# Reciprocals of the softmax row sums: spread by a DRAM round trip instead of on VectorE

## The chip, the cores and the metric

One core of one Trainium2 chip runs the whole program. The metric is the device time of one execution in microseconds (us). The kernel before takes 999.54 us (median of three runs, 999.5 to 1000.05).

## What is computed

The reference is one cross-attention block with adaptive layer norm, 16 images, 1024 query rows, 64 context rows and 16 heads of 32 features, all in float32:

```python
xq  = ada_ln(x_q,  t_vec, Wss_q,  bss_q)      # (1 + scale) * layernorm + bias
xkv = ada_ln(x_kv, t_vec, Wss_kv, bss_kv)
q   = (xq @ Wq + bq).reshape(B, Lq, 16, 32)   # B 16, Lq 1024, H 512
k, v = (xkv @ Wkv + bkv) split in 16 heads    # Lkv 64
attn = softmax(q k^T / sqrt(32))
return x_q + (attn v).reshape(B, Lq, 512) @ Wp + bp
```

The change concerns the division of softmax: every head and query row has one sum of exponentials, and `attn v` is multiplied with its reciprocal.

## The kernel before

**Tiles.** The 16 x 1024 query rows are cut into NB = 32 blocks of 512 rows (TB). Block `i` passes through a pipeline that is spread over several iterations of one loop (`for i in range(3, NB - 2)`, 27 iterations). The order of the instructions on each engine is written out by hand; each engine executes its own in that order. An iteration works at once on: scores and exponentials of block `i`; the multiplication with v, the division and half of the output projection of block `a = i - 1`; the rest of the projection of `b = i - 2`; the query projection of `n = i + 1`; the scaling of the features of `f = i + 2`; layer norm and turning of `i + 3` and the statistics of `i + 4`.

**Scores and weights.** 128 partitions hold 4 groups `c` of 32 context rows, the columns are 4 heads `r` in the group by 512 query rows. TensorE writes the scores `ps` (L738), VectorE takes a maximum over 32x32 blocks (L755) and spreads it to the tile `mb` (L784), GpSimd subtracts (L797), ScalarE takes the exponential (L808).

**The row sums.** GpSimd adds the two halves of the exponentials to the tile `sum` (`total`, L858). Its buffer has the tag `vb` and is one of its kind. VectorE sums it by blocks to `lt` (`row_total`, L863), 128 partitions by 64 columns: partition 32c + a and column (r, j) hold the sum of head (c, r), query row 32j + a.

**The reciprocals.** `inverse_rows` (L875) takes the reciprocal of `lt` (L878), writes it to DRAM (L881), and reads it back in four pieces (L883) such that partition 32r + a holds what belongs to head position `r`, as 64 columns (c, j), tile `vr`. One iteration later `spread_rows` (L886, the instruction at L891) makes the 128x2048 tile `vb` of it on VectorE: a 32x32 transpose of each column repeated 32 times. `divided` (L915) multiplies `po`, the weights times v that TensorE left in PSUM, with `vb` and leaves `ot`, of which the output projection is made.

**The queues.** Almost all DMAs are issued by SyncE (SP), in program order. After `total(i)` these are, in an iteration: the next block's x (L119), two copies `p<-s` (`swapped`, L813, each 32 partitions of 8 KB), twelve moves `xt<-ht` (L382, each 32 partitions of 2 KB) of block `i + 3`, then the write and the four reads of `inverse_rows`, then the last four moves, the next block's residual `r` (L126) and two stores of a finished block (L1118). The moves bring the turned features to the tile `xt`. Of that tile ScalarE scales one chunk after another in the next iteration (`scale_features(f, ...)`, L442), and each chunk has all 128 partitions, thus needs all sixteen moves. In ScalarE's order the first of the four scales stands ahead of `biased(a, 2)` (L1031) and of both exponentials (L808) of block `i`.

Of the kernel before, what the change touches and what calls it, by code (L numbers as in the profile page):

```python
# [9 lines left out]
F32 = mybir.dt.float32  # L10
# [5 lines left out]
P = 128  # L16
# [4 lines left out]
def cross_attention_block(  # L21
# [18 lines left out]
    nc = tc.nc  # L40
# [5 lines left out]
    NC = H // P  # L46
    HPC = P // DH
    TB = 512
    NT = TB // P
    BPB = LQ // TB  # L50
    NB = B * BPB
# [8 lines left out]
    qpool = ctx.enter_context(tc.tile_pool(name="qpool", bufs=2))  # L60
# [5 lines left out]
    dram = ctx.enter_context(tc.tile_pool(name="dram", bufs=2, space=bass.MemoryType.DRAM))  # L66
# [518 lines left out]
    def quarter_products(i, v, first):  # L585

        x, t, k = feature_quarter(i, v), t_quarters, 1 if v == 7 else 0
        w = lambda m, c: weight_quarter(v, m, c)
        s = lambda k: weight_quarter_sum(v, k)
        if first:  # L590
            qa["q", k] = bank(f"pq_{i}_{v}", k)
            todo = (
                (0, w(0, 0), x[:, 0, 0, :]),
                (1, s(0), t[:, 0]),
                (2, s(2), t[:, 1]),
                (3, s(1), t[:, 2]),
            )
        else:
            todo = (
                (0, w(0, 1), x[:, 0, 1, :]),  # L600
                (1, s(3), x[:, 1, 1, :]),
                (2, w(1, 1), t[:, 3]),
            )
        for q, lhsT, rhs in todo:
            nc.tensor.matmul(  # L605
                qa["q", k][:, q * P : (q + 1) * P],
                lhsT=lhsT,
                rhs=rhs,
                start=first and q == 0,
                stop=True,  # L610
                skip_group_check=True,
            )
# [150 lines left out]
    def copied(i, z, e):  # L763
        nc.scalar.copy(s_tiles[i, z][:, 2 * e : 2 * e + 2, :], s_banks[i, z][e])  # L764
# [69 lines left out]
    vb_tiles = {}  # L834
# [40 lines left out]
    def inverse_rows(i):  # L875

        lt = lt_tiles.pop(i)
        nc.vector.reciprocal(lt, lt)  # L878
        v = small.tile([P, NC, NJ], F32, tag="vr", name=f"vr_{i}", bufs=2)
        d = dram.tile([NC, 32, HPC, NJ], F32, tag="lt", name=f"ltd_{i}")  # L880
        nc.sync.dma_start(d.rearrange("c a r j -> (c a) r j"), lt)  # L881
        for r in range(HPC):
            nc.sync.dma_start(v[32 * r : 32 * r + 32], d[:, :, r, :].rearrange("c a j -> a c j"))  # L883
        vt_rows[i] = v

    def spread_rows(i, cs=range(NC)):  # L886
        n = len(cs)
        v = vt_rows[i][:, cs[0] : cs[-1] + 1, :].rearrange("p c j -> p (c j)")
        if cs[0] == 0:
            vb_tiles[i] = qpool.tile([P, NC, TB], F32, tag="vb", name=f"vb_{i}", bufs=1)  # L890
        nc.vector.transpose(  # L891
            vb_tiles[i][:, cs[0] : cs[-1] + 1, :].rearrange("p c q -> p (c q)"),
            v.unsqueeze(2).to_broadcast([P, n * NJ, 32]),
        )
        if cs[-1] == NC - 1:
            vt_rows.pop(i)
# [198 lines left out]
    def added(i, n):  # L1095

        m, o = {1: (0, 0), 2: (0, 0), 6: (0, 1), 7: (1, 1), 5: (1, 1), 4: (0, 1), 3: (1, 0)}[n]
        r = r_tiles[i][:, 2 * m : 2 * m + 2, o * HO : (o + 1) * HO]
        k = acc_bank(i, n)
        if i < NB - 1 or n not in (1, 6, 5, 3):  # L1100
            a = acc[k].rearrange("p (t h) -> p t h", t=2)
        if i == NB - 1:

            for ts in ((0,), (1,)) if n in (1, 6, 5, 3) else ((0, 1),):
                src = z_halves[ts[0]][:, :HO].unsqueeze(1) if len(ts) == 1 else a
                ts = slice(ts[0], ts[-1] + 1)
                nc.vector.tensor_add(r[:, ts, :], src, r[:, ts, :])  # L1107
                if n == 5 and ts.start == 0:
                    continue
                if n == 5:  # L1110
                    ts = slice(0, 2)
                if n in (2, 3, 4, 5):
                    dst = rows_of(out, i)[:, 2 * m : 2 * m + 2, o * HO : (o + 1) * HO]
                    nc.sync.dma_start(dst[:, ts, :], r[:, ts, :])
            return
        nc.vector.tensor_add(r, a, r)  # L1116
        if n in (3, 4):
            nc.sync.dma_start(  # L1118
                rows_of(out, i)[:, 2 * m : 2 * m + 2, :], r_tiles[i][:, 2 * m : 2 * m + 2, :]
            )  # L1120
# [298 lines left out]
    context_out("B", "v", 7)  # L1419
    hidden(4, (2,))  # L1420
    inverse_rows(0)
    maximum(1, 1, 0)
    feature_sums(2, nc.gpsimd, (0,))
# [96 lines left out]
    added(0, 7)  # L1520
    feature_sums(3, nc.gpsimd, (3,))
    inverse_rows(1)
    added(0, 6)
    again(1, 1)
# [55 lines left out]
    move(5, ks=(2,))  # L1580
    row_total(2)
    inverse_rows(2)
    move(5, ks=(3,))
    feature_sums(4, nc.gpsimd, (3,))
    load_residual(2)

    for i in range(3, NB - 2):
        a, b, n, f = i - 1, i - 2, i + 1, i + 2
# [37 lines left out]
        product(b, 3)  # L1626
        quarter_adds(n, 7)
        quarter_products(n, 7, False)
        spread_rows(a)
        added(b, 4)  # L1630
        if i < NB - 3:
            hidden(i + 3, (3,))
# [72 lines left out]
    y, z = NB - 2, NB - 1  # L1705
# [29 lines left out]
    query_added(z, 4)  # L1735
    added(y - 2, 7)
    copied(y, 1, 0)
    spread_rows(y - 1)
    copied(y, 1, 1)
    subtract(y, zs=(1,))  # L1740
    query_out(z, 3)
# [127 lines left out]
```

## Time and profile before

| | before |
|---|---|
| median of the runs | 999.54 us |
| the profiled execution | 999.71 us, of it the span 997.9 us |
| TensorE (PE) busy | 984.6 us, 99% of the span |
| VectorE (DVE) busy | 896.2 us, 90% |
| GpSimd (POOL) busy | 894.6 us, 90% |
| ScalarE (ACT) busy | 778.1 us, 78% |
| the spread at L891, 33 times | 73.8 us of VectorE, 2238 ns each |
| DMA of the hardware queue (q1) | 163.93 MB, 55.3% of 16 engines |

Busy time is the time in which an engine had an instruction of the program; the idle time in front of an instruction is shown in brackets with what ended it. "SPq" rows are the issues of DMAs: their duration is the time that the issue took, not the transfer. A DMA's landing is told by the profile as a median from issue to the completion of its last byte. Matmul ends are modelled, so a busy TensorE must be read beside the regularity of its starts.

### The profile page before, as it was taken

How to read it: one execution, taken by the hardware profiler on the slowest of the kernel's cores; microseconds unless marked ns; L12 is line 12 of the kernel's file. 1: busy time of each engine (PE TensorE's matmuls, PEld its weight loads, DVE VectorE, ACT ScalarE, POOL GpSimd, SP SyncE). 2: the span in 40 equal slices, each digit the busy share in tenths (PEclk: the TensorE clock that was granted, in tenths of full speed). 3: DMA queues.
4: the chain of work that ended last, by engine and by line, in shares of the span. 5: the costliest groups of instructions: out<-in, count | busy, mean ns of one | idle time of the engine just before them, and what ended most of it. 6: DMA issues, size and time to landing. Idle time of an engine off the chain costs nothing.

```text
span 997.9 us, 20561 instructions
## 1 busy us (share of the span) xinstructions
PE 984.6 (99%) x7465; PEld 762.7 (76%) x7465; DVE 896.2 (90%) x1318; ACT 778.1 (78%) x1165; POOL 894.6 (90%) x690
## 2 busy tenths in 40 slices
PE   7999999999999999999999999999999999999997
PEld 7888777787777877877778778777787787777756
DVE  6787889999999999999999999999999999987786
ACT  3788778888888888888888888888888888876620
POOL 3668899999999999999999999999999999999681
PEclk9999999999999999999999999999999999999999
DMA  9665736555655455466555554665555555444422
GB/s 314 233 195 149 191 90 178 152 164 182 188 177 175 154 176 150 148 187 188 180 176 150 175 158 141 187 187 181 173 153 174 147 155 183 147 136 133 142 81 97
DMA packets 115188, 165.77 MB, mean 166 GB/s; under 512 B 34920, under 2 KB 46464, under 8 KB 113168
## 3 DMA queue, kind: packets, MB, share of 16 engines
q1 hardware_dynamic: 114704, 163.93, 55.3%
q8 instruction: 59, 0.97, 0.4%
q0 software_dynamic: 384, 0.54, 0.2%
q14 instruction: 41, 0.34, 0.1%
HBM read 79.47 MB, written 34.60 MB: 114 GB/s over the span
## 4 chain that ended last, share of the span: by engine, by line
PE 93%; DVE 3%; DMA 1%; issue 1%; SPq 0%; ACT 0%; DVEq 0%; ACTq 0%
PE pp L1086 36%; PE pq L534 30%; PE pq L605 10%; PE ps L738 7%; PE po L936 6%; PE pv_B L534 1%; PE pk_B L534 1%; PE pk_A L534 1%; PE pv_A L534 1%; DMA vr<-ltd 0%; DMA ltd<-lt 0%; DVE vb L891 0%; DVE m L755 0%; DVE xk_sums_A L493 0%; DVE l L826 0%
## 5 line engine op out<-in xcount | busy, mean ns | idle before, releaser
L797 POOL TENSOR_TENSOR s<-s,mb 128x2048 f32<-128x2048 f32 x64 | 290.6, 4563 | 20.3 <-DVE mb L784 12.3
L1086 PE MATMUL pp<-w_p_sb,ot 128*128 128x256 f32 x740 | 174.8, 380 | 1.2 <-DVE ot L915 1.2
L764 ACT COPY s<-ps 128x1024 f32<-128x1024 f32 x128 | 129.3, 1012 | 58.2 <-PE ps L738 46.5
L755 DVE TRANSPOSE_TENSOR_REDUCE m<-ps 128x32 f32<-128x1024 f32 x128 | 152.6, 1228 | 12.0 <-PE ps L738 11.5
L1086 PEld LDWEIGHTS pp<-w_p_sb,ot 128*128 128x128 f32 x740 | 138.6, 190 | 19.8 <-issue 1.8
L858 POOL TENSOR_TENSOR sum<-s,p 128x2048 f32<-128x2048 f32 x30 | 136.3, 4544 | 1.5 <-ACT p L808 1.5
L645 ACT ACTIVATE qt<-pq,bias_t 128x256 f32<-128x256 f32 x256 | 107.2, 471 | 34.2 <-PE pq L605 27.8
L1116 DVE TENSOR_TENSOR r<-pp,r 128x512 f32<-128x512 f32 x183 | 120.3, 669 | 13.6 <-ACT xt L442 5.8
L534 PE MATMUL pq<-xt,w_q_sums 128*128 128x256 f32 x512 | 123.8, 385 | 0.0
L534 PEld LDWEIGHTS pq<-xt,w_q_sums 128*128 128x128 f32 x512 | 95.1, 190 | 34.4 <-issue 22.6
L1086 PE MATMUL pp<-WT,ot 128*128 128x256 f32 x492 | 118.4, 384 | 0.0
L1086 PE MATMUL pp<-WT,s 128*128 128x256 f32 x488 | 116.1, 381 | 1.2 <-DVE r L1107 0.8
L817 ACT ACTIVATE s<-s 32x2048 f32<-32x2048 f32 x60 | 114.6, 1910 | 1.4
L1086 PEld LDWEIGHTS pp<-WT,ot 128*128 128x128 f32 x492 | 91.1, 190 | 18.3 <-issue 3.6
L327 ACT ACTIVATE x<-x,rstdq 128x512 f32<-128x512 f32 x128 | 94.8, 807 | 5.0 <-POOL rstdq L304 5.0
L1086 PEld LDWEIGHTS pp<-WT,s 128*128 128x128 f32 x488 | 88.3, 191 | 13.4 <-DVE r L1107 1.2
L442 ACT ACTIVATE xt<-xt,ss_q 128x512 f32<-128x512 f32 x124 | 94.4, 808 | 1.1 <-DMA xt<-ht 1.0
L915 DVE TENSOR_TENSOR ot<-po,vb 128x1024 f32<-128x1024 f32 x62 | 73.0, 1218 | 15.9 <-PE po L936 15.6
L493 POOL TENSOR_TENSOR xt_sums<-xt 128x512 f32<-128x512 f32 x64 | 81.2, 1268 | 6.2 <-ACT xt L442 6.0
L286 DVE BATCH_NORM_STATS2 bs<-x 128x6 f32<-128x512 f32 x128 | 85.3, 666 | 0.0
L891 DVE STREAM_TRANSPOSE vb<-vr 128x2048 f32<-128x2048 f32 (+1 forms) x33 | 73.8, 2238 | 6.2 <-DMA vr<-ltd 6.0
L357 DVE STREAM_TRANSPOSE ht<-x 128x512 f32<-128x512 f32 x124 | 77.5, 679 | 0.4 <-issue 0.2
(224 smaller groups left out, 1964.5 us busy)
## 6 DMA issues: line engine op xcount, KB each, us to landing
x<-in_x_dram SPq DMA_DIRECT2D x32, 1024.0 KB, 5.5
r<-in_x_dram SPq DMA_DIRECT2D x32, 1024.0 KB, 5.7
xt<-ht SPq DMA_DIRECT2D x488, 64.0 KB, 2.0
out_dram<-r SPq DMA_DIRECT2D x60, 512.0 KB, 4.8
p<-s SPq DMA_DIRECT2D x60, 256.0 KB, 3.8
wss_kv<-in_L_xcond_Wss_kv_dram SPq DMA_DIRECT2D x4, 512.0 KB, 7.2
wss_q<-in_L_xcond_Wss_q_dram SPq DMA_DIRECT2D x4, 512.0 KB, 11.6
vr<-ltd SPq DMA_DIRECT2D x128, 8.0 KB, 1.7
```

Source lines behind the costliest of these rows:

```text
L327: nc.scalar.activation(dst, src, AF.Identity, bias=rstd[:, 1, j : j + 1], scale=rstd[:, 0, j : j + 1])
L442: nc.scalar.activation(xt[:, :, c, :], xt[:, :, c, :], AF.Identity, scale=ss["q"][:, c, b : b + 1], bias=ss["q"][:, NC + c, b : b + 1],)
L534: nc.tensor.matmul(out_, lhsT=lhsT, rhs=rhs, start=new and m == 0 and c == 0, stop=c == HC - 1, skip_group_check=True,)
L605: nc.tensor.matmul(qa["q", k][:, q * P : (q + 1) * P], lhsT=lhsT, rhs=rhs, start=first and q == 0, stop=True, skip_group_check=True,)
L645: nc.scalar.activation(dst, src, AF.Identity, bias=bq_t[:, o : o + 1])
L755: nc.vector.tensor_reduce(m_tiles[i][:, z, 2 * e : 2 * e + 2, :], s_banks[i, z][e].rearrange("p r (j a) -> p r j a", a=32), AX.X, ALU.max, ...
L764: nc.scalar.copy(s_tiles[i, z][:, 2 * e : 2 * e + 2, :], s_banks[i, z][e])
L797: eng.tensor_tensor(s_tiles[i, z], s_tiles[i, z], mb_tiles[i], ALU.subtract)
L817: nc.scalar.activation(s_tiles[i, 0][at + 32 : at + 64], raw_tiles[i][at : at + 32], AF.Exp, scale=SCALE)
L858: nc.gpsimd.tensor_tensor(t, s_tiles[i, 0], s_tiles[i, 1], ALU.add)
L1086: nc.tensor.matmul(to, lhsT=rows[:, c, t * P : (t + 1) * P], rhs=cols[:, c, :], start=n == 2 and (i, 2) not in seeded and t == 0 and c == ...
L1116: nc.vector.tensor_add(r, a, r)
```

## The change

For blocks 2 to 29 `inverse_rows` now takes another way, and `spread_rows` is not called for them (in the loop, and once behind it). VectorE transposes the 128x64 reciprocals in 32x32 blocks, so that a partition holds 32 query rows that lie side by side. One DMA writes them to DRAM as whole rows of 512 floats, 256 pieces of 128 bytes. Four DMAs read them back: each takes the four rows (2 KB each) of one head position `r` and writes them to all 32 partitions of its quarter of `vb`. `vb` is thus filled at the end of iteration `i` by DMA, and not in iteration `i + 1` by VectorE. Blocks 0, 1, 30 and 31 keep the old way.

```diff
         v = small.tile([P, NC, NJ], F32, tag="vr", name=f"vr_{i}", bufs=2)
+        if 2 <= i < NB - 2:
+            t = v.rearrange("p c j -> p (c j)")
+            nc.vector.transpose(t, lt.rearrange("p r j -> p (r j)"))
+            d = dram.tile([2, NC, 2, TB], F32, tag="lb", name=f"lb_{i}")
+            nc.sync.dma_start(
+                d.rearrange("k c e (j a) -> (c e j) k a", a=32),
+                t.rearrange("p (k a) -> p k a", k=2),
+            )
+            vb = vb_tiles[i] = qpool.tile([P, NC, TB], F32, tag="vb", name=f"vb_{i}", bufs=1)
+            for r in range(HPC):
+                row = d[r // 2, :, r % 2, :].unsqueeze(0)
+                nc.sync.dma_start(vb[32 * r : 32 * r + 32], row.to_broadcast([32, NC, TB]))
+            return
         d = dram.tile([NC, 32, HPC, NJ], F32, tag="lt", name=f"ltd_{i}")
...
         quarter_products(n, 7, False)
-        spread_rows(a)
         added(b, 4)
...
     copied(y, 1, 0)
-    spread_rows(y - 1)
     copied(y, 1, 1)
```

What the instruction order becomes is shown at three places, around the iteration that works on block 14. On VectorE, where the spread stood, before (`pq_7` is the query projection of the next block, `r_4253` a block whose projection is being added, `po` the weights times v of block 13):

```order
L624 TENSOR_TENSOR pq_7_4623<-pq_7_4623,t_quarters 128x128
L891 STREAM_TRANSPOSE vb_4654<-vr_4510 128x2048
L1116 TENSOR_TENSOR r_4253<-pp_3_4490,r_4253 128x2x256
L1116 TENSOR_TENSOR r_4253<-pp_2_4427,r_4253 128x2x256
L915 TENSOR_TENSOR ot_4686<-po_0_4662,vb_4654 128x1024
L915 TENSOR_TENSOR ot_4686<-po_1_4663,vb_4654 128x1024
```

and after:

```order
L624 TENSOR_TENSOR pq_7_4625<-pq_7_4625,t_quarters 128x128
L1129 TENSOR_TENSOR r_4255<-pp_3_4490,r_4255 128x2x256
L1129 TENSOR_TENSOR r_4255<-pp_2_4427,r_4255 128x2x256
L928 TENSOR_TENSOR ot_4686<-po_0_4662,vb_4514 128x1024
L928 TENSOR_TENSOR ot_4686<-po_1_4663,vb_4514 128x1024
```

The spread is gone, and the division (L915 before, L928 after) reads a `vb` of an earlier number, one filled by DMA in the iteration before. On VectorE, at the reciprocal at the end of the iteration, before:

```order
L863 TENSOR_REDUCE lt_4777<-sum_4722 128x64
L878 RECIPROCAL lt_4777<-lt_4777 128x64
L755 TENSOR_REDUCE m_15_4820<-ps_0_0_4802 128x32
L755 TENSOR_REDUCE m_15_4820<-ps_0_1_4803 128x32
L622 TENSOR_TENSOR t_quarters<-pq_1_4823,t_quarters 128x128
```

and after:

```order
L863 TENSOR_REDUCE lt_4777<-sum_4722 128x64
L878 RECIPROCAL lt_4777<-lt_4777 128x64
L882 STREAM_TRANSPOSE vr_4780<-lt_4777 128x64
L755 TENSOR_REDUCE m_15_4822<-ps_0_0_4804 128x32
L755 TENSOR_REDUCE m_15_4822<-ps_0_1_4805 128x32
L622 TENSOR_TENSOR t_quarters<-pq_1_4825,t_quarters 128x128
```

A transpose of 128x64 stands between the reciprocal and the maxima of the next block's scores. On SyncE, between the copies `p<-s` and the stores, before (each of the four reads of 8 KB):

```order
L813 DMA p_4439<-s_0_4281 32x2048 x2
L382 DMA xt_4462<-ht_4425 32x512 x12
L881 DMA ltd_4511<-lt_4507 128x64
L883 DMA vr_4510<-ltd_4511 32x4x16 x4
L382 DMA xt_4462<-ht_4425 32x512 x4
L126 DMA r_4523<-in_x_dram 128x4x512
```

and after (each of the four reads of 256 KB into SBUF):

```order
L813 DMA p_4439<-s_0_4283 32x2048 x2
L382 DMA xt_4462<-ht_4425 32x512 x12
L884 DMA lb_4512<-vr_4510 128x2x32
L891 DMA vb_4514<-lb_4512 32x4x512 x4
L382 DMA xt_4462<-ht_4425 32x512 x4
L126 DMA r_4525<-in_x_dram 128x4x512
```

The places in the queue stay; what stands ahead of the last four moves is now 1 MB in place of 32 KB.

## The prediction

> **What bounds the kernel now.** I read the page's busy shares first, then busy time by stretch for the loop, then the long chain.
>
> ```profile
> PE 984.6 (99%) x7465; PEld 762.7 (76%) x7465; DVE 896.2 (90%) x1318; ACT 778.1 (78%) x1165; POOL 894.6 (90%) x690
> ...
> 180.00:893.00 713.00, 713.00 (x5502) 554.35 (x5501) 671.95 (x968) 598.37 (x871) 687.69 (x527) 1.00 0.56 166
> ...
> 188.13 3.45 PE pq L534 x16
> ...
> 901.15 3.45 PE pq L534 x16
> ```
>
> In the loop TensorE has 713.00 us of work in 713.00 us, at full clock. The same piece of the chain, a query product, starts at 188.13 and, 25 iterations later, at 901.15: 28.52 us each. TensorE sets this period. VectorE (671.95) and POOL (687.69) have 41 and 25 us to spare, 1.6 and 1.0 us an iteration. So time taken from VectorE is worth nothing here, and the question is what the added work makes late. Rings of work that pass from one iteration to the next must close in under 28.52 us; I look for those with little room.
>
> **Part 1, the spread removed: nothing.** It is 28 instructions:
>
> ```profile
> L891 DVE STREAM_TRANSPOSE vb<-vr 128x2048 f32<-128x2048 f32 (+1 forms) x33 | 73.8, 2238 | 6.2 <-DMA vr<-ltd 6.0
> ...
> 569.33 2.36 DVE L915 TENSOR_TENSOR ot<-po,vb 128x1024 f32<-128x1024 f32 x2 [0.65 <-PE po L936]
> ...
> 938.10 2.30 DVE L891 STREAM_TRANSPOSE vb<-vr 128x2048 f32<-128x2048 f32 x1
> 940.32 0.65 DVE L1116 TENSOR_TENSOR r<-pp,r 128x512 f32<-128x512 f32 x1
> ...
> 938.35 1.89 PE L1086 MATMUL pp<-WT,s 128*128 128x256 f32 x8
> ```
>
> At 2.30 us each these would be 28 x 2.30 = 64 us of VectorE, but the division behind the spread waits for TensorE's `po` already (0.65 us idle at 569.33); that idle becomes about 2.9 us. Behind the loop the spread at 938.10 is followed by an addition that needs a product of TensorE which runs from 938.35 to 940.24, so it would start at 940.25 instead of 940.32. I count 0.
>
> **Part 2, the small transpose: nothing, with little room.** It has no row before. The nearest are the transposes of 128x512 and 128x2048:
>
> ```profile
> L357 DVE STREAM_TRANSPOSE ht<-x 128x512 f32<-128x512 f32 x124 | 77.5, 679 | 0.4 <-issue 0.2
> L784 DVE STREAM_TRANSPOSE mb<-m 128x2048 f32<-128x2048 f32 x32 | 74.0, 2311 | 1.2
> ...
> 577.90 2.31 DVE L863 TRANSPOSE_TENSOR_REDUCE lt<-sum 128x64 f32<-128x2048 f32 x1
> 580.25 0.55 DVE L878 RECIPROCAL lt<-lt 128x64 f32<-128x64 f32 x1
> 581.14 2.38 DVE L755 TRANSPOSE_TENSOR_REDUCE m<-ps 128x32 f32<-128x1024 f32 x2 [0.33 <-PE ps L738]
> ```
>
> The line through them is (2311 - 679) / 1536 = 1.06 ns a column and 135 ns fixed, so 64 columns take an estimated 0.20 us. From below it is bounded by the fixed part, 0.13, from above by the reciprocal of the same shape, 0.55. VectorE idles 0.33 us at this place for TensorE's scores, so 0.20 fits and 0.55 would make the maxima 0.22 us late. Queued behind them are the quarter sums and the spread of `mb`, for which TensorE and POOL wait. I take 0.20: cost 0, but the room in this ring shrinks from 0.33 to about 0.13 us.
>
> **Part 3, the DMAs.** SyncE in one iteration, what ScalarE and POOL do with the moves' result, and what DMAs take:
>
> ```profile
> 549.40 1.15 SPq L813 DMA_DIRECT2D p<-s  x2
> 550.64 8.57 SPq L382 DMA_DIRECT2D xt<-ht  x12
> 559.31 0.53 SPq L881 DMA_DIRECT2D ltd<-lt  x1
> 560.98 1.75 SPq L883 DMA_DIRECT2D vr<-ltd  x4
> 562.77 2.41 SPq L382 DMA_DIRECT2D xt<-ht  x4
> ...
> 568.13 0.81 ACT L442 ACTIVATE xt<-xt,ss_q 128x512 f32<-128x512 f32 x1
> 568.84 0.59 ACT L1031 COPY pp<-b_p_sb 128x512 f32<-128x512 f32 x1
> 569.35 1.92 ACT L808 ACTIVATE s<-s 128x2048 f32<-128x2048 f32 x1
> 571.16 1.91 ACT L808 ACTIVATE p<-s 128x2048 f32<-128x2048 f32 x1
> ...
> 573.32 4.55 POOL L858 TENSOR_TENSOR sum<-s,p 128x2048 f32<-128x2048 f32 x1
> ...
> x<-in_x_dram SPq DMA_DIRECT2D x32, 1024.0 KB, 5.5
> xt<-ht SPq DMA_DIRECT2D x488, 64.0 KB, 2.0
> p<-s SPq DMA_DIRECT2D x60, 256.0 KB, 3.8
> vr<-ltd SPq DMA_DIRECT2D x128, 8.0 KB, 1.7
> ```
>
> This is a ring: `sum` ends, SyncE copies `p<-s`, issues twelve moves, writes, waits for the write, issues four reads and the last four moves; these land; ScalarE scales (L442), copies, takes two exponentials to 573.07; POOL adds `sum` from 573.32. SyncE is busy nearly all of it. Room in it: before, the last move (562.77 + 2.41 - 0.60 = 564.6 issued, 2.0 to land) is there at 566.6, and ScalarE comes to it at 568.13, 1.5 us later; then 573.32 - 573.07, about 0.2 with the hand-over, at POOL.
>
> The write: 32 KB in 256 pieces in place of 128; bounds 0 and the 0.53 of its issue once more; I take 0. The issue of four reads: 0.42 each before, 0.58 for `p<-s`; 0 to 0.6 us. The data decide. The four reads put 1 MB ahead of 256 KB of moves into one queue, whose order the profile shows (the move at 550.64, first behind `p<-s`, takes the longest of all in the loop to land, 4.8 us against a median of 2.0; the row is below). How fast is it? Two stretches with the engines nearly always busy, first a load of x to 128 partitions, then `p<-s`, which reads and writes 32 partitions a piece:
>
> ```profile
> DMA packets 374, 0.76 MB, mean 382 GB/s; under 512 B 1, under 2 KB 1, under 8 KB 374
> ...
> DMA packets 124, 0.57 MB, mean 239 GB/s; under 512 B 36, under 2 KB 36, under 8 KB 60
> ...
> L382 SPq DMA_DIRECT2D xt<-ht x401: 507/589/1865, 180.9 to 892.9; - x134
> ...
> DMA to landing us min/median/max: 1.9/2.0/4.8
> ```
>
> The reads come from DRAM as x does but write to 32 partitions as `p<-s` does. Call X the time from the first read's issue to the last move's landing. The fixed part is a move's 2.0 less its 0.3 of data, 1.7. At the x rate, with the 5.5 us that a whole 1 MB of x takes and 0.7 for the moves, X = 6.2; at 195 GB/s (two `p<-s` with 0.57 between issues: 0.57 + 3.8 - 1.7 = 2.7 us for 0.52 MB) X = 1.7 + 1.31 / 0.195 = 8.4. These are the bounds. I take the 32-partition write to be the limit, 225 GB/s between 195 and 239: X = 1.7 + 5.8 = 7.5. Before it was 564.6 - 561.0 + 2.0 = 5.6.
>
> The Trainium skill speaks to this choice ("SBUF — State Buffer", section "Door 1: The DMA port swizzle"): 32 neighbouring partitions lie on 8 of 16 ports, and a 1 MiB transfer to them was measured at 189 GB/s. By it, X would be an estimated 1.7 + 6.9 = 8.6. The trace agrees for `p<-s` (239 against 382); no run here shows it yet for a load from DRAM.
>
> How much time is there? From the first read's issue to ScalarE's first scale:
>
> ```profile
> 163.25 1.75 SPq L883 DMA_DIRECT2D vr<-ltd  x4
> 169.07 0.81 ACT L442 ACTIVATE xt<-xt,ss_q 128x512 f32<-128x512 f32 x1
> ...
> 902.86 1.76 SPq L883 DMA_DIRECT2D vr<-ltd  x4
> 910.38 0.81 ACT L442 ACTIVATE xt<-xt,ss_q 128x512 f32<-128x512 f32 x1
> ...
> 619.27 1.74 SPq L883 DMA_DIRECT2D vr<-ltd  x4
> 625.17 0.81 ACT L442 ACTIVATE xt<-xt,ss_q 128x512 f32<-128x512 f32 x1
> ```
>
> Of 27 such pairs the first has 5.8 and the last 7.5 us; SyncE's issues vary (619.27: 5.9), the mean of all is 7.0. With 0.2 at POOL the ring closes in time up to X = 7.2 on average. At 7.5 it is 0.3 us too long, and once the 0.1 to 0.3 us at the maxima is used up, lateness adds from iteration to iteration: 27 x 0.3 = 8 us. Followed pair by pair, lateness carried on, the 27 give 9 us, since a wide pair gives nothing back while TensorE sets the pace. The sum: 999.7 (profiled execution, its span 997.9 and 1.8 around it) + 9 = **1008.7 us**; the profiled execution is 0.2 above the median of the runs, 999.54, which I leave aside.
>
> Is `vb` itself in time? It lands at 1.7 + 1.05 / 0.225 = 6.4 us behind the first read, and the division comes at 569.33 - 560.98 = 8.35. Queued later on SyncE are the residual, needed an iteration on, and stores.
>
> **Rivals.**
> - *In time after all (not slower).* If the reads run at the x rate, X is 6.2 to 6.6: under 7.0, and only the first and the tightest pair lose some tenths. The engines' work is hidden, time 999.5 to 1001. For it: 382 GB/s, and that DRAM is the source; against it: every transfer to 32 partitions in this trace is slower. It decides from X below 7.1.
> - *`vb` itself late.* Should 32 reads of one DRAM row be slow (a bias row read to 128 partitions at the start gives no sign of that), `vb` lands past 8.35 us; each us late stops TensorE, which needs `ot` at once: 28 us for each, thus 1030 and more.
> - *The small transpose is dear.* At 0.55 it passes the 0.33 us by 0.22: 27 x 0.2 = 6 us, 1005.5.
> - *Faster.* Were VectorE the bound, 28 x 2.2 = 62 us would go, 938. The 713.00 of 713.00 speaks against it; a gain of 2 us would need gaps of TensorE that the trace doesn't show.
>
> **How the numbers follow.** Forecast (the ring of moves too long) 0.56, in time 0.31, `vb` late 0.05, transpose dear 0.05, faster 0.03. About 0.2%, 2 us, is what a measurement of this kernel can tell from no change. Slower: 0.56 + 0.05 + 0.05 = 0.66; same 0.31; faster 0.03. The forecast's own range: followed in the same way X of 7.2 gives 4 us and X of 7.9 gives 19, so 1003 to 1019. For 8 in 10 I reach down over the case in time to 999 and up to 1020.
>
> **What would show it.** Right: ScalarE's first L442 of an iteration waits for the DMA `xt<-ht` in most iterations (before: 0.3 us in all); the four reads move some 220 GB/s; TensorE shows idle time or longer waits in the loop, the query product's starts lie 28.8 to 29 us apart, and VectorE's idle time before the division grows to about 2.9 us. Wrong: no waits at L442 and 28.52 us still (in time after all); idle at the division ended by a DMA (`vb` late); the maxima waiting for nothing while L882 takes over 0.33 us (the transpose).

## The result, and the profile after

The changed kernel takes 1050.06 us (median of four runs, 1046.58 to 1051.37) against 999.52 us for the kernel before beside it: a ratio of 1.0496, 95% interval 1.0481 to 1.051. It is slower, as forecast, but by 50 us and not by 9; 1050 lies outside the range of 999 to 1020. The profiled execution took 1050.21 us, its span 1048.4.

Which engine sets the end? The busy shares of the page, and the loop by stretch:

```profile
PE 1004.1 (96%) x7465; PEld 760.4 (73%) x7465; DVE 839.7 (80%) x1318; ACT 782.4 (75%) x1165; POOL 896.3 (85%) x690
...
180.00:893.00 713.00, 687.97 (x5194) 520.46 (x5193) 588.30 (x918) 567.91 (x827) 647.92 (x501) 1.00 0.70 191
```

In the stretch in which TensorE was busy for 713.00 of 713.00 us it now is for 687.97, at the same full clock. VectorE lost 56.5 us of work (896.2 to 839.7), and the time did not fall. The share by engine of the chain that ended last, from the page before and then from the page after:

```profile
PE 93%; DVE 3%; DMA 1%; issue 1%; SPq 0%; ACT 0%; DVEq 0%; ACTq 0%
```

```profile
POOL 29%; PE 27%; DVE 12%; issue 10%; SPq 9%; DMA 7%; ACT 4%; POOLq 0%; ACTq 0%; DVEq 0%
```

TensorE no longer leads this chain; it passes through POOL, ScalarE, VectorE, SyncE and the DMAs, which is what a ring looks like when it sets the period. Where the waits are, in the loop (us in all, times, longest):

```profile
ACT xt L442 <- DMA xt<-ht: 51.5, 24, 3.5
POOL sum L858 <- ACT p L808: 44.9, 24, 3.3
DVE ot L928 <- PE po L949: 40.2, 21, 2.1
PEld pp L1099 <- ACT pp L1044: 23.4, 23, 2.3
DVE ot L928 <- DMA vb<-lb: 10.3, 4, 2.9
```

(Lines behind the added code stand 13 further down than before: L915 is now L928, L1086 L1099, L1031 L1044.) ScalarE's first L442 waits for the moves in 24 iterations, 51.5 us in all. Before, the same view of the loop had

```profile
ACT xt L442 <- DMA xt<-ht: 0.3, 1, 0.3
```

POOL's `sum` inherits the wait (44.9), and so does TensorE's projection by way of the bias copy (23.4). The spread's place is now idle time for `po` (40.2): VectorE waits for TensorE, as forecast. In four iterations `vb` itself comes last.

One turn of the ring, from the timeline (start, duration, engine, line):

```profile
541.03 4.54 POOL L858 TENSOR_TENSOR sum<-s,p 128x2048 f32<-128x2048 f32 x1 [1.84 <-ACT p L808]
...
557.10 2.61 SPq L891 DMA_DIRECT2D vb<-lb  x4
559.75 2.42 SPq L382 DMA_DIRECT2D xt<-ht  x4
...
566.50 0.81 ACT L442 ACTIVATE xt<-xt,ss_q 128x512 f32<-128x512 f32 x1 [2.31 <-DMA xt<-ht]
...
569.54 1.89 ACT L808 ACTIVATE p<-s 128x2048 f32<-128x2048 f32 x1
...
571.51 4.53 POOL L858 TENSOR_TENSOR sum<-s,p 128x2048 f32<-128x2048 f32 x1 [2.12 <-DMA out_dram<-r]
```

`sum` runs 4.54 us; from its end to the first read 11.53; from the read to ScalarE's scale 9.40; from there to the next `sum` 5.01: 30.48 us, against 28.52 us, TensorE's turn before. (The last releaser is a case of a wait put down to the wrong name: `sum` follows the exponential, which ends at 571.43.) Over the loop's 27 turns the mean from the end of `sum` to the first read is 11.82 us (11.68 before), and from the read to the scale 9.03 (7.05 before). With 5.0 and 4.53 the turn is 30.4 us, 1.87 over TensorE's 28.52, and 27 x 1.87 = 50 us: the whole loss. The first and last start of `sum`, before and then after, say the same:

```profile
L858 POOL TENSOR_TENSOR sum<-s,p x30: 4529/4544/4558, 86.6 to 915.6; 128x2048 f32<-128x2048 f32 x30
```

```profile
L858 POOL TENSOR_TENSOR sum<-s,p x30: 4520/4533/4553, 86.2 to 966.5; 128x2048 f32<-128x2048 f32 x30
```

829.0 us have become 880.3, 51.3 more, so neither the start nor the end of the program contributes.

The queue in that turn, microsecond by microsecond from the first read's issue (length of the stretch; busy time of PE, PEld, DVE, ACT and POOL; clock; share of the 16 DMA engines; GB/s):

```profile
557.10:558.10 1.00, 1.00 (x6) 0.90 (x5) 1.00 (x3) 1.00 (x3) 0.83 (x2) 1.00 0.10 25
558.10:559.10 1.00, 1.00 (x10) 0.97 (x10) 0.97 (x4) 1.00 (x3) 1.00 (x1) 1.00 0.92 285
559.10:560.10 1.00, 1.00 (x6) 0.88 (x6) 0.96 (x3) 0.97 (x3) 1.00 (x1) 1.00 1.08 197
560.10:561.10 1.00, 1.00 (x6) 0.89 (x5) 0.93 (x4) 1.00 (x3) 1.00 (x1) 1.00 1.03 217
561.10:562.10 1.00, 1.00 (x7) 0.87 (x6) 0.82 (x2) 1.00 (x2) 1.00 (x1) 1.00 1.05 209
562.10:563.10 1.00, 1.00 (x9) 0.95 (x7) 0.42 (x1) 0.33 (x1) 1.00 (x2) 1.00 1.06 195
563.10:564.10 1.00, 1.00 (x18) 0.35 (x25) 0.28 (x1) 0.75 (x2) 1.00 (x1) 1.00 1.08 187
564.10:565.10 1.00, 1.00 (x24) 0.15 (x8) 0.00 (x0) 0.09 (x1) 1.00 (x1) 1.00 0.91 176
565.10:566.10 1.00, 1.00 (x13) 0.88 (x6) 0.82 (x1) 0.00 (x0) 1.00 (x1) 1.00 1.05 352
```

From 558.10 to 565.10 the share is 0.91 to 1.08, that of 16 busy engines, and after the first microsecond they move 176 to 217 GB/s. In the last row, where the residual is read behind the moves, they move 352 at the same share. So the engines are not idle for want of work: the reads and the moves hold them longer per byte. (The last rows also show TensorE still at work while ScalarE stands still; it is out of work later, with 0.26 us of busy time from 567.10 to 568.10.)

The trace also keeps, for each of these DMAs, the times of sixteen completions: a DMA lands in sixteen parts, and has landed with the last. As medians over the 27 turns, from the first read's issue, the eighth part of the four reads is complete at 2.95, 4.25, 5.47 and 6.81 us, thus 1.29 us apart, which is 204 GB/s, and that of the last move at 8.06. The last part comes later: 7.42 for the last read, 8.62 for the last move (8.86 as a mean).

### The profile page after: what moved, and what is told of

Its sections match the earlier page's. It is cut to its first block, busy times and chain, and to the rows that moved or that the text cites. A ratio compares the mean times of both kernels' runs of the same rounds, so it can differ in the third digit from the quotient of the medians.

```text
span 1048.4 us, 20534 instructions
## 1 busy us (share of the span) xinstructions
PE 1004.1 (96%) x7465; PEld 760.4 (73%) x7465; DVE 839.7 (80%) x1318; ACT 782.4 (75%) x1165; POOL 896.3 (85%) x690
## 4 chain that ended last, share of the span: by engine, by line
POOL 29%; PE 27%; DVE 12%; issue 10%; SPq 9%; DMA 7%; ACT 4%; POOLq 0%; ACTq 0%; DVEq 0%
POOL s L797 16%; POOL sum L858 10%; PE pq L534 9%; PE pp L1099 7%; SPq L382 7%; DVE lt L863 4%; PE ps L738 4%; DVE m L755 3%; DMA xt<-ht 2%; DMA r<-in_x_dram 2%; ACT s L764 2%; POOL s L1064 2%; DMA lb<-vr 2%; PE pq L605 2%; SPq L891 1%
## 5 line engine op out<-in xcount | busy, mean ns | idle before, releaser
L1099 PE MATMUL pp<-w_p_sb,ot 128*128 128x256 f32 x740 | 180.8, 388 | 29.3 <-ACT pp L1044 17.6
L1129 DVE TENSOR_TENSOR r<-pp,r 128x512 f32<-128x512 f32 x183 | 123.7, 676 | 76.2 <-PE pp L1099 72.6
L1099 PEld LDWEIGHTS pp<-w_p_sb,ot 128*128 128x128 f32 x740 | 134.3, 190 | 66.2 <-ACT pp L1044 28.2
L442 ACT ACTIVATE xt<-xt,ss_q 128x512 f32<-128x512 f32 x124 | 94.3, 807 | 60.6 <-DMA xt<-ht 60.6
L1099 PE MATMUL pp<-WT,ot 128*128 128x256 f32 x492 | 118.3, 383 | 0.0
L928 DVE TENSOR_TENSOR ot<-po,vb 128x1024 f32<-128x1024 f32 x62 | 73.0, 1219 | 55.7 <-PE po L949 40.2
L1099 PE MATMUL pp<-WT,s 128*128 128x256 f32 x488 | 116.1, 380 | 1.0 <-DVE r L1120 0.8
L1099 PEld LDWEIGHTS pp<-WT,ot 128*128 128x128 f32 x492 | 91.0, 190 | 18.4 <-issue 5.6
L1099 PEld LDWEIGHTS pp<-WT,s 128*128 128x128 f32 x488 | 88.2, 190 | 13.2 <-issue 1.7
L863 DVE TRANSPOSE_TENSOR_REDUCE lt<-sum 128x64 f32<-128x2048 f32 x31 | 71.6, 2309 | 19.2 <-POOL sum L858 19.2
```

Source lines behind the costliest of these rows:

```text
L442: nc.scalar.activation(xt[:, :, c, :], xt[:, :, c, :], AF.Identity, scale=ss["q"][:, c, b : b + 1], bias=ss["q"][:, NC + c, b : b + 1],)
L863: nc.vector.tensor_reduce(lt_tiles[i], sum_tiles.pop(i).rearrange("p r (j a) -> p r j a", a=32), AX.X, ALU.add, apply_transpose=True,)
L1099: nc.tensor.matmul(to, lhsT=rows[:, c, t * P : (t + 1) * P], rhs=cols[:, c, :], start=n == 2 and (i, 2) not in seeded and t == 0 and c == ...
```

## The experiments

The theory to be tested has two halves. *The ring:* time is lost because the last four moves stand behind the reads in one queue, and only from the point at which X, the time from the first read's issue to the last move's landing, passes some 7 us. *The rate:* X is as long as it is because of where the reads write. Rivals: removing the spread or adding the transpose costs something of its own; the DRAM rows, each read 32 times, are slow; a fixed cost (the write's round trip, the issues), not the bytes, makes X long; the place in the loop slows any load.

### The spread and the transpose by themselves

The kernel before without its spread, no DMA added; the division reads the 64 reciprocals of a partition 32 times each:

```diff
-        spread_rows(a)
...
+                v = vb[:, cs, :].rearrange("p c j -> p (c j)").unsqueeze(2)
+                    v.to_broadcast([P, n * NJ, 32]),
```

> The kernel before with the spread on VectorE left out for blocks 2 to 29 and no DMA added: the division reads the 64 columns of vr, each 32 times, so that it multiplies with other values than it should; its instructions keep their number and size. Theory A and the prediction: TensorE sets the pace and the spread was hidden, 998.5 to 1000.5 us; idle time of VectorE before the division grows from 0.65 to about 2.9 us. Rival (VectorE was a bound, and the change has a gain of its own that the DMAs eat): 940 to 990 us.

Measured: 999.77 us, ratio 1.000 (0.999 to 1.001). Its busy shares, and the wait ahead of the division in the loop, here and then in the kernel before:

```profile
PE 987.0 (99%) x7465; PEld 762.9 (76%) x7465; DVE 836.9 (84%) x1290; ACT 777.8 (78%) x1165; POOL 895.2 (89%) x690
...
DVE ot L919 <- PE po L950: 47.6, 25, 1.9
```

```profile
DVE ot L915 <- PE po L936: 14.8, 23, 1.1
```

59 us of VectorE are gone, and the time is the same. The idle time before the division grew from 14.8 to 47.6 us, which is 1.9 us an iteration; the rest became idle time elsewhere. The spread was free: with TensorE at 99%, nothing was to be gained by removing it.

And the kernel before with the small transpose added to it:

```diff
+        if 2 <= i < NB - 2:
+            nc.vector.transpose(v.rearrange("p c j -> p (c j)"), lt.rearrange("p r j -> p (r j)"))
```

> The kernel before, complete, with the small transpose of the reciprocals added behind the reciprocal in the loop; its result goes to vr and is overwritten by the four reads, the spread is still there. If the transpose (0.245 us in the changed kernel's trace) fits in the 0.33 us for which VectorE waited there: 999 to 1001. If it makes the maxima late in each iteration: 1003 to 1007.

Measured: 1000.2 us, ratio 1.0002 (0.9991 to 1.0013). VectorE's wait for the scores in the loop of the kernel before, and then the transpose in this run, all of them and one with the maxima behind it:

```profile
DVE m L755 <- PE ps L738: 6.4, 21, 0.4
```

```profile
L881 DVE STREAM_TRANSPOSE vr<-lt x28: 245/245/246, 153.6 to 923.3; 128x64 f32<-128x64 f32 x28
...
581.10 0.24 DVE L881 STREAM_TRANSPOSE vr<-lt 128x64 f32<-128x64 f32 x1
581.34 2.38 DVE L755 TRANSPOSE_TENSOR_REDUCE m<-ps 128x32 f32<-128x1024 f32 x2
```

It fits, but only just: the wait of the maxima behind the reciprocal was 0.27 us on average in the loop of the kernel before, and 0.02 us of it are left. Free too. What remains is the DMAs.

### The moves ahead of the reads

The changed kernel with the last four moves issued between the write and the reads:

```diff
             move(i + 3, ks=(3,))
+        read_rows(i)
```

> The change, with the last four moves issued between the write and the four reads of vb; nothing is left out. Theory A (the moves of xt stand in the queue behind 1 MB of vb, and ScalarE's first scale waits for them): the moves land as in the kernel before, the waits of L442 on the DMA xt<-ht fall from 51.5 us in the loop to under 5, and the loss shrinks to what a vb that comes 1.3 us later costs at the division, some 0.2 to 0.5 us an iteration: 1003 to 1015 us. Theory B (vb's own lateness at the division makes the loss): vb lands later than in the change, so the loss grows, over 1060. Theory C (DMA load as such slows SyncE, ScalarE or the moves): no change, 1045 to 1055.

Measured: 1024.27 us, ratio 1.0237 (1.0219 to 1.0255). ScalarE's wait for the moves is gone from the list of waits altogether; in its place stands, in that kernel's list:

```profile
DVE ot L934 <- DMA vb<-lb: 74.0, 25, 3.7
```

The moves do hold the ring up, and freeing them gives back half of the 50 us. But the reads, issued 1.4 us later now, still take 7.5 us from the first issue to the last landing, and the division waits for them: 74.0 us in 25 iterations, 3.0 us each, where it waited 1.9 us for `po` in the run without the spread. 24 us of time are left, 0.9 us an iteration. The expected 1003 to 1015 was missed because `vb`'s own lateness had been thought small. Both places at which the data are used have too little room; in the order of the change the moves happen to be the tighter one.

### Fewer bytes

If the bytes make X long, fewer of them must close the ring, at a point that can be said beforehand. `vb` of three, then of two column blocks in place of four (`n` is 3 or 2):

```diff
-                row = d[r // 2, :, r % 2, :].unsqueeze(0)
-                nc.sync.dma_start(vb[32 * r : 32 * r + 32], row.to_broadcast([32, NC, TB]))
+                row = d[r // 2, :n, r % 2, :].unsqueeze(0)
+                nc.sync.dma_start(vb[32 * r : 32 * r + 32], row.to_broadcast([32, n, TB]))
```

> The changed kernel with vb of three column blocks in place of four: each of the four reads brings 6 KB in place of 8 KB to each of its 32 partitions (0.79 MB in all), the issues, the write, the transpose and the moves stay; the second division takes column blocks 1 and 2, so the last columns are divided by the wrong rows' sums: part of the computation left out. Ring theory (bytes at some 184 GB/s set X, and the loop is longer by X less 7.0 us, times 27): the reads land 1.7 + 0.79/0.184 = 6.0 us after the first read's issue, the last move 1.3 later, X = 7.3, time 1003 to 1013. Rival (a fixed cost sets it: the write's round trip, four more issues, the shared row): 1040 to 1050.

Measured: 1008.49 us, ratio 1.009 (1.0075 to 1.0105).

> As the run with three column blocks, with two: 4 KB to each partition, 0.52 MB in all; both divisions take the same two blocks, so half the columns are divided by the wrong sums. Ring theory: reads land 1.7 + 0.52/0.184 = 4.6 us after the first issue, last move 5.9, below the 7.0 that fit: 999 to 1001.5, waits for the moves at L442 almost gone. Rival (fixed cost): 1030 to 1050.

Measured: 1000.48 us, ratio 1.0012 (1.0003 to 1.0021). ScalarE's wait for the moves, first with three quarters, then with half of the bytes:

```profile
ACT xt L442 <- DMA xt<-ht: 16.3, 20, 2.0
```

```profile
ACT xt L442 <- DMA xt<-ht: 0.7, 1, 0.7
```

51.5, 16.3 and 0.7 us, and a time that goes with them, both as expected: the bytes do it, and the write's round trip, its wait and the four issues, which are all still there with half the bytes, do not make the ring too long by themselves. The reads' last landing, as a median over the 27 turns, is 4.35, 5.99 and 7.42 us after the first issue for 0.52, 0.79 and 1.05 MB: about 1.3 us and 5.9 us a megabyte, or 171 GB/s.

### Where the bytes come from

Three of the four reads take distinct rows of `x` in place of one row 32 times; `vb` is wrong, all else stays:

```diff
+                if r > 0:
+                    rows = x[i // BPB].rearrange("(p c z) h -> p c z h", p=32, c=NC)[:, :, r, :]
```

> The change, with three of the four reads of vb taken from x in DRAM, 32 partitions by four separate pieces of 2 KB, in place of one row read 32 times; sizes, destinations and waits stay, so three quarters of vb hold other values than they should. Theory A1 (the write to 32 partitions limits the rate): the reads still move about 200 GB/s, 1042 to 1055 us. Theory A2 (16 engines that read the same 8 KB of DRAM limit it): near the 382 GB/s of a load of x, the moves land 6.2 to 6.6 us after the first read's issue, 999 to 1005 us.

Measured: 1055.2 us, ratio 1.0552 (1.0534 to 1.0569); the reads land at 7.50 us (7.42 in the change). That is at the upper end of the first theory's range, 0.2 us above it. Reading one DRAM row 32 times is not what is slow.

### Where they go to

The first attempts sent each read to all 128 partitions, 2 KB to each.

```diff
-                row = d[r // 2, :, r % 2, :].unsqueeze(0)
-                nc.sync.dma_start(vb[32 * r : 32 * r + 32], row.to_broadcast([32, NC, TB]))
+                row = d[0, r, 0, :].unsqueeze(0)
+                nc.sync.dma_start(vb[:, r, :], row.to_broadcast([P, TB]))
```

> The change, with the four reads of 256 KB each going to all 128 partitions by 2 KB (one row of DRAM 128 times) in place of 32 partitions by 8 KB; bytes and pieces stay, vb holds other values than it should. Theory A1 (32 partitions limit the rate): about 380 GB/s, the moves land 6.2 to 6.8 us after the first read's issue, 999 to 1004 us. Theory A2 (the common source limits): still about 200 GB/s, 1042 to 1060 us.

Measured: 1031.61 us, ratio 1.0311 (1.0284 to 1.0337). A miss by both theories: part of the loss went, and most of it stayed. One row now went to 128 partitions, so the source was changed too; with three of the four reads taken from `x`:

```diff
-                nc.sync.dma_start(vb[:, r, :], row.to_broadcast([P, TB]))
+                rows = d[0, r, 0, :].unsqueeze(0).to_broadcast([P, TB])
+                if r > 0:
+                    rows = x[i // BPB].rearrange("(p z) h -> p z h", p=P)[:, r, :]
+                nc.sync.dma_start(vb[:, r, :], rows)
```

> The changed kernel with each of the four reads going to all 128 partitions, 2 KB each, and three of the four taking distinct rows of x as source (the first one DRAM row of the sums, to 128 partitions), so vb holds wrong numbers; bytes, number of issues and the write as in the change. If the 32-partition destination limits the changed kernel and the single hot source row limited the run before with 128 partitions: the reads run near the x load's 382 GB/s, land 4.5 to 5.2 us after the first issue, last move 5.5 to 6.5, time 999 to 1004. If loads from DRAM beside the other traffic run at some 210 GB/s whatever the destination: last move 7.8 to 8.8, time 1030 to 1050.

Measured: 1043.42 us, ratio 1.0438 (1.0411 to 1.0465). That is in the range of the second theory, that loads at this place of the loop are slow whatever they write to. With nearly all the bytes in one DMA of `x`:

```diff
+            nc.sync.dma_start(vb[0:32, 0, :], d[0, 0, 0, :].unsqueeze(0).to_broadcast([32, TB]))
+            rows = x[i // BPB].rearrange("(p z) h -> p z h", p=P)
+            nc.sync.dma_start(vb[:, 1:, :], rows[:, 1:NC, :])
+            nc.sync.dma_start(vb[32:, 0, :], rows[32:, 0, :])
```

> The changed kernel with vb filled by three reads: 64 KB of the sums' row to partitions 0 to 31 (so that the wait for the write stays), then 0.79 MB of x in one DMA to all 128 partitions, then the last 0.2 MB of x to partitions 32 to 127. vb holds wrong numbers but for the first piece; the bytes are those of the change, one issue fewer. If the rate is a matter of the destination's partitions (all 128 as in the x load): some 380 GB/s, landed 4.6 to 5.3 us after the first issue, last move 5.6 to 6.3, 999 to 1002. If loads at this place of the loop run at 215 GB/s whatever they write to: last move 8 to 8.8, 1025 to 1050.

Measured: 1029.75 us, ratio 1.0295 (1.0268 to 1.0323). Again in between. All three mix a broadcast row or unequal DMAs into the comparison, so a pair was made with the same source and other destinations: the same 1 MB of `x` in four DMAs, behind a small read that keeps the wait for the write. (One more thing differs: the trace has packets of 8 KB in the first twin and of 2 KB in the second.) The second twin against the first:

```diff
             nc.sync.dma_start(v[0:1].rearrange("p c j -> p (c j)"), d[0:1, 0, 0, 0 : NC * NJ])
             rows = x[i // BPB].rearrange("(p z) h -> p z h", p=P)
             for r in range(HPC):
-                ps = slice(32 * r, 32 * r + 32)
-                nc.sync.dma_start(vb[ps], rows[ps, :NC, :])
+                nc.sync.dma_start(vb[:, r, :], rows[:, r, :])
```

> The changed kernel with a read of one 256-byte row of the sums into vr, which nothing uses and which keeps SyncE's wait for the write, and then four reads of x to vb, 32 partitions each, 8 KB to each partition: vb holds wrong numbers. The first of a pair that differs in the destination alone: all 1 MB comes from distinct rows of x in four DMAs, no row is read twice. If 32 partitions set the rate: the four land 7.4 to 7.8 us after the small read's issue, the last move about 9.1, 1050 to 1065. It is the same by the other theory; the difference from its twin counts.

> The twin: the same small read and the same 1 MB of x in four DMAs, but each to all 128 partitions, 2 KB to each. If 32 partitions set the rate of the changed kernel: the four land 5.5 to 6.4 us after the small read's issue, the last move 7.0 to 7.8, 1000 to 1018, so 40 us or more under its twin. If the place in the loop, or the cut into four DMAs, sets the rate whatever the destination: within 10 us of its twin.

Measured: 1054.33 us to 32 partitions each (ratio 1.0545, 1.0522 to 1.0567), 1026.2 us to 128 (1.0263, 1.0241 to 1.0285). Three turns of each, 1.5 to 5 us behind the first read of `x` (length, VectorE's busy time, clock, share of the DMA engines, GB/s), 32 partitions first:

```profile
500.69:504.19 3.50, 2.74 (x7) 1.00 1.03 239
530.94:534.44 3.50, 2.80 (x7) 1.00 1.03 234
561.78:565.28 3.50, 2.67 (x7) 1.00 1.05 246
```

```profile
489.55:493.05 3.50, 2.97 (x8) 1.00 0.95 304
518.30:521.80 3.50, 2.80 (x7) 1.00 0.94 297
547.11:550.61 3.50, 2.77 (x7) 1.00 0.80 245
```

239, 234, 246 against 304, 297, 245 GB/s (three more turns of each have 229 to 239 against 297 to 308), and the landings, 7.45 against 6.71 us after the small read (medians of 27 turns): the destination is worth 28 of the 54 us. The size of the packets doesn't explain it: the run with three reads of `x` to 32 partitions, further above, has packets of 2 KB too, and 1055.2 us. The twin missed its own expected 1000 to 1018, so the destination is not all of it. The sixteen completions show where the rest lies. In the first twin the last read's parts are complete between 6.84 and 7.45 us, close together. In the second they are complete between 4.80 and 6.71 us: the eighth, at 5.61, is 5.3 us behind the first read of `x`, nearly as fast as the load of `x` elsewhere in the loop (5.1), but the last is 1.1 us behind the eighth (0.5 there). And then come the moves, which write 32 partitions each; the last of them is complete another 1.1 us later.

The Trainium skill ("SBUF — State Buffer", section "Door 1: The DMA port swizzle") has 32 neighbouring partitions on 8 of 16 ports, and partitions 0 to 63 on other ports than 64 to 127. The pair agrees with the first in direction: 32 partitions were slower. The second would let reads to the two halves overlap, if they follow each other; so the order 0, 64, 32, 96 was tried, with `x` as source and in the change itself:

```diff
-            for r in range(HPC):
+            for r in (0, 2, 1, 3):
```

> As e14_x_32, the four reads in the order partitions 0, 64, 32, 96, so that lower and upper 64 follow each other in turn. If the DMA engines run far enough apart to write to both halves at once: 10 to 30 us less than e14_x_32. If they go through the DMAs in step: within 5 us of it.

> The changed kernel, complete, with its four reads in the order partitions 0, 64, 32, 96. If the engines write to both halves at once: 1020 to 1040. If they go through the DMAs in step: 1047 to 1053, as the change.

Measured: 1045.99 us (ratio 1.0465, 1.0447 to 1.0482) where the plain order had 1054.33, and 1042.4 us (1.0423, 1.0407 to 1.0438) where the change had 1050.06. 8 us each time, outside the intervals, but less than the 10 that the expectation asked for: as if the halves overlapped a little. In the completions of the last run the eighth parts of successive reads are 1.20 us apart in place of 1.29, thus 218 in place of 204 GB/s: the order made the reads themselves faster. That it is by an overlap of the halves is not shown.

### A run that measured something else

To have 64 partitions on both halves, reads of one column block to partitions 32 to 95 were set against the same to 0 to 63:

```diff
+            for c in range(NC):
+                rows = d[0, c]
+                nc.sync.dma_start(vb[0:64, c, :], rows.unsqueeze(1).to_broadcast([2, 32, TB]))
+            for r in (2, 3):
```

> The changed kernel, complete, with the first two reads (partitions 0 to 31 and 32 to 63, 8 KB each) cut the other way: four reads of one column block each to partitions 0 to 63 (2 KB each), then partitions 64 to 95 and 96 to 127 as before: six issues in place of four, the same bytes. It is the control of the run with partitions 32 to 95. If the ports behind a partition number set the rate (neighbours 0 to 63 share eight of sixteen, as 0 to 31 do): some 215 GB/s still, the last move 8.7 to 9.1 us after the first issue, 1045 to 1058. If 64 partitions are simply better than 32: half the bytes at 300 or more, 1016 to 1030, and no difference from its twin.

And the twin:

```diff
+                rows = d.rearrange("k c e t -> (k c e) t")[2 * c + 1 : 2 * c + 9 : 7]
+                nc.sync.dma_start(vb[32:96, c, :], rows.unsqueeze(1).to_broadcast([2, 32, TB]))
+            for r in (0, 3):
```

> The twin of the run before it, complete: four reads of one column block each to partitions 32 to 95, then 0 to 31 and 96 to 127; the same six issues, pieces and bytes, only other destination partitions. If the upper and the lower 64 partitions have ports of their own: the first 0.52 MB go at 300 to 380 in place of some 205 GB/s, which saves 0.8 to 1.2 us of the 8.8, and 22 to 32 us of time: 1016 to 1030. If the source (rows shared by 32 partitions) or the number of pieces sets the rate: within 4 us of its twin.

Measured: 1375.88 us (ratio 1.3753, 1.3723 to 1.3782) and 1358.61 us (1.3588, 1.3562 to 1.3614): no theory's number. The first of the two, in the stretch after its reads were issued at 629.48 (columns as in the nine rows of the change above):

```profile
638.50:640.00 1.50, 1.09 (x6) 0.61 (x4) 0.00 (x0) 0.00 (x0) 0.68 (x1) 1.00 0.13 46
640.50:642.00 1.50, 0.00 (x0) 0.00 (x0) 0.00 (x0) 0.00 (x0) 0.00 (x0) 1.00 0.14 52
...
644.00:646.00 2.00, 0.00 (x0) 0.00 (x0) 0.00 (x0) 0.00 (x0) 0.00 (x0) 0.50 0.98 295
```

A share of 0.13 is 2 engines of 16, at an estimated 23 to 26 GB/s each. The source of these reads has an outer dimension of two (two rows, each repeated 32 times). That agrees with the Trainium skill ("DMA: Bandwidth & Descriptors", section "Rules for kernel authors"), by which an outermost dimension of size c under 16 confines a DMA to at most c engines. For the question of the halves the pair is void.

### The ring's rule against all runs

ScalarE's first scale, counted from the first read's issue (mean of 27 turns), against the profiled execution's time. The rule is the prediction's, with the scale in place of X: in time up to 7.2 us, beyond that 27 times the excess on top of 999.7.

| run | scale at, us | rule, us | profiled execution, us |
|---|---|---|---|
| half the bytes | 6.86 | 999.7 | 1002.85 |
| three quarters | 7.51 | 1008.1 | 1009.37 |
| `x` to 128 partitions | 8.05 | 1022.7 | 1024.09 |
| one row to 128 partitions | 8.21 | 1027.0 | 1027.63 |
| mostly one DMA of `x` | 8.27 | 1028.6 | 1027.53 |
| order 0, 64, 32, 96 | 8.77 | 1042.1 | 1044.11 |
| `x` mostly, four DMAs to 128 | 8.84 | 1044.0 | 1045.15 |
| `x` to 32, order 0, 64, 32, 96 | 8.86 | 1044.5 | 1044.02 |
| **the change** | 9.03 | 1049.1 | 1050.21 |
| `x` to 32 partitions | 9.11 | 1051.3 | 1052.71 |
| mostly `x`, 32 partitions | 9.15 | 1052.4 | 1053.58 |

Ten of eleven lie within 2.1 us of it; the first profiled execution was 2.4 us above its own runs' median of 1000.48. Once the ring sets the period, the scale's time is one part of that period; so the table confirms the point from which it counts and that the rest of the turn stays as it was, and not what makes X long.

## Why the prediction was right or wrong

**What bounds the kernel** was right: TensorE's 28.52 us are the floor, and only a ring longer than that costs.

**Part 1, nothing for the spread,** was right; the run without it shows it. The division's idle time did take its place, at 1.9 us an iteration where the forecast had 2.9; nothing hangs on the difference.

**Part 2, 0.20 us for the transpose at no cost,** was right: 0.245 us each in the change, and no loss by itself. The room left at the maxima was put at 0.13 us; it was 0.02.

**Part 3, the ring of moves,** was right in its place, its direction and its room. 7.2 us and 27 times the excess, taken from before alone, fit ten of the eleven runs of the table within 2.1 us.

**What failed is the size of X in part 3: 7.5 us were taken, 8.6 measured** (median of 27 turns; 8.9 as a mean). The formula was 1.7 + 1.31 MB / 225 GB/s. The step in it that failed is "the 32-partition write to be the limit, 225 GB/s between 195 and 239". That limit was at work, for 28 of 54 us in the pair of `x`, but the rate was too high, and the formula has no term for the time between the parts of a DMA. The completions show both, for the mean of 8.86:

- *The rate.* The reads follow each other at 204 GB/s. 1.31 MB / 204 GB/s = 6.4 us in place of 5.8; with the fixed 1.7 that is 8.1, and the eighth part of the last move is there at 8.06. This is 0.6 us of the error.
- *The parts don't end together.* The fifteenth part of the last move comes at 8.42, 0.36 us behind the eighth; this too is missing from the formula.
- *One late part.* The sixteenth is mostly there at once, but in seven of the 27 turns it comes 0.85 to 1.95 us behind the fifteenth, 9.4 us in all. In each of the seven, a packet of 16 KB of the kind that the page calls `instruction` ran between the first read's issue and the fifteenth part, for 0.93 to 1.37 us (in five other turns it ran there with a lag of at most 0.5 us). That it held up the late part is thus likely; no run tests it.

Besides X, two times that the forecast put at nothing count in each turn: 0.16 us from the last landing to ScalarE's scale, and 0.14 us more from the end of `sum` to the first read (11.82 against 11.68), where the write stands.

An error of 1.4 us in X is multiplied by 27 once the room is used up: with those two times, and within the rounding of these means, the excess of 0.3 us became 1.87, and 9 us became 50. The forecast stood just above a threshold, where the time is most sensitive to the term that was known worst, and its own bounds for X went to 8.4, which by the same rule is 27 x 1.2 = 32 us and 1032. The range followed X only up to 7.9, without a reason for stopping there, so its 1020 didn't hold the forecast's own bound.

The estimate from the Trainium skill ("SBUF — State Buffer", section "Door 1: The DMA port swizzle": 189 GB/s into 32 neighbouring partitions, an X of 8.6) was the better one: measured 8.6. Its case was nearer to the operation, a transfer of a whole megabyte to 32 partitions, while the rows it was weighed against were those of `p<-s`, of half a megabyte. That it fits so closely is in part luck: here 204 GB/s and parts that end apart make up the sum that it gives with one rate.

**The rivals.** *In time after all* would have needed the rate of `x`; half the bytes show that point, at 1000.5. *`vb` itself late* was held unlikely at 28 us for each us late; its place was real: four turns of the change show it, and with the moves ahead it is what the division waits for in every turn. Its price was about right: there the first read is issued 1.6 us later than before (13.24 against 11.68 us behind `sum`) and lands 7.6 us on, thus some 0.8 us past the 8.35, which makes 22 us, and 24 were measured. *The transpose dear* and *faster* fell with parts 1 and 2.

**What stays open.** With 128 partitions as destination, 26 us of the loss remain. The middle part of the reads is then nearly as fast as in the load of `x` elsewhere in the loop; the last part and the moves make the rest. Why the sixteen parts end some 1.9 us apart there was not settled. Nor was it why the run with one broadcast row and three reads of `x` to 128 partitions (1043.42) is slower than the runs with four broadcast rows (1031.61) and with none (1026.2).

## What to carry to other kernels

Before work is moved from an engine to a DMA queue, ask what is queued behind it: here a transfer of 1 MB that nothing waited for soon delayed 256 KB that everything waited for. Write each ring's length against the bound engine's period; below it a change is free, beyond it every tenth counts once per iteration, so a forecast near that threshold needs the range of its worst-known term carried through the multiplication. And price a transfer by its destination's partitions and by the landing of its last part, not by the mean rate that a queue shows.

## What was not expected of the hardware

- Reads whose source has two rows, each repeated 32 times, ran at 46 to 52 GB/s with 0.13 to 0.14 of the DMA engines busy, and such reads made the kernel 1.36 to 1.38 times as long.
- In the first of the two runs with such reads TensorE had nothing to do from 640 to 650 us, and its granted clock stood at 0.50 in 644 to 646 us (the row above); over that whole execution it was 0.883. TensorE's busy time was 1056.5 us there, for the 7465 instructions that took 984.6 in the kernel before: such a stall was paid twice, by the wait and by the slower work behind it. In the change itself the waits were short and the clock was 0.998 over the whole.
- The order in which four reads follow each other in one queue (0, 64, 32, 96 for 0, 32, 64, 96) was worth 8 us of 1050, with two different sources.
- In seven of the change's 27 turns, one of the sixteen parts of the last move landed 0.85 to 1.95 us behind the others, each time with a 16 KB packet of the kind `instruction` in the same stretch.
